# Layer 1's last group of hidden values: seven half-size products per half of the tokens in place of eight row pieces, and one comparison on ScalarE

## The chip, the cores and the metric

The kernel runs on one core of one Trainium2 chip, in one launch. The metric is device microseconds of that core, the median of the runs. Before the change it is 1847.09 us (three runs, 1846.87 to 1848.96).

A core has five engines that work side by side, each through its own queue in order: TensorE (PE, with its weight loads as PEld), VectorE (DVE), ScalarE (ACT), GpSimd (POOL) and SyncE (SP), whose queue here issues nearly all DMA transfers. Waits between engines are semaphore waits at the head of a queue, so that what stands behind a waiting instruction waits too.

## What is computed

Two layers over 2 x 1024 tokens of width 512, in fp32. Each layer adds to `x` an attention-like branch and an MLP-like branch of the normalised `x`. The change is in the last part, layer 1's second branch:

```python
def _sparsify_2to4(h):
    B, S, I = h.shape
    g = h.reshape(B, S, I // 4, 4)
    a = jnp.abs(g)
    _, idx = jax.lax.top_k(a, 2)
    pos = jnp.arange(4)
    mask = (pos == idx[..., 0:1]) | (pos == idx[..., 1:2])
    return (g * mask.astype(g.dtype)).reshape(B, S, I)
h = jax.nn.silu(jnp.einsum('bsh,hi->bsi', x, w_gate)) * jnp.einsum('bsh,hi->bsi', x, w_up)
h_sparse = _sparsify_2to4(h)
return jnp.einsum('bsi,ih->bsh', h_sparse, w_down)
```

So of every four neighbouring hidden values the two largest in size are kept, and the result is multiplied with `w_down` and added to `x`.

## The kernel before, in words

**Staging.** The kernel has three stages: layer 0 (pool `a`), layer 1's attention (pool `b`), and layer 1's second branch (pool `c`, from the end of attention on). Only the third matters here. `in_program_order` fixes each engine's order to the order in which the instructions are written, so the queues are an order written out by hand.

**The third stage.** The tokens are taken in two halves of 1024 (`pb`), and the 2048 hidden values in four groups of 512 (`g`). That makes eight groups, numbered 0 to 7 in the order of the work, and each is built by two of the 16 "units". A unit computes gate and up for 1024 tokens with seven products in place of eight (`gate_up`, line 179 for the matmuls, with a form of Strassen's method). Group 7 belongs to units 14 and 15, and is the last. `gate_up` calls `hook(0)` to `hook(6)` between its products; `put1(unit, at, ...)` hangs work of earlier groups into these hooks. What doesn't fit goes into the list `tail`, which is run after unit 15, item by item.

**Sparsification** (`sparsify`, L1385 to L1414) is a generator of twelve steps for one half of a group's tokens (512 of its 1024): the absolute value on ScalarE (L1399), then eleven on VectorE: the smaller of each pair (L1400), two comparisons within the pair (L1402, L1403), the larger (L1404), two comparisons across the pairs (L1406, L1407), their difference (L1408), two updates of the mask (L1409, L1410) and twice the multiplication of the hidden values with the mask (L1414, two of the four members each). `some_steps(n, half, count)` runs the next `count` steps.

**The down projection** comes in two forms:

- By seven products (`down_by_seven`, L246 to L325): for one half of the tokens, the hidden values and the weights are each cut into four quarters; sums of quarters are formed (of hidden values on VectorE, `hidden_first` and `hidden_last`, L265, L266, L272, L273; of weights on GpSimd, `down_weights`, L1373 to L1378), and seven products of 4 matmuls (128x256) are run (L297). Product 0 is copied by ScalarE (L304), product 1 added to it by VectorE (L307), which gives u2; products 2 to 6 are added to `x` by VectorE (L310), and u2 is added to three quarters of `x` by GpSimd (`add_u2`, L315). The products of a half take turns in two PSUM banks: `(m + half) % 2` for products 0, 1, 3 and 4, and 2, 5 and 6 go on in the bank of 0, 3 and 4.
- Row by row (`row_down`, L1454): for 128 tokens, four matmuls of 128x512 into one bank of the wide PSUM tiles, one addition to `x` by VectorE (L1459), and for the last group one store of these rows (L1462).

Groups 0 to 5 go by seven products in both halves. Group 6 goes by seven in half 0 and by four row pieces in half 1. Group 7 goes by eight row pieces. For group 6, `own_t3` (L1383) makes one weight difference apart, so that the weights themselves stay whole for the row pieces; it takes a tile of the tag `td1`, which has two buffers.

**The tail before** is the rest of group 6 (five products of half 0, each preceded by a row piece of half 1 as long as there are any), with the steps of group 7's sparsification between them by the list `steps`, and then group 7's eight row pieces, the first four on half 0 and the others on half 1.

Of the kernel before, what the change touches and what calls it, by code (L numbers as in the profile page):

```python
# [11 lines left out]
AF = mybir.ActivationFunctionType  # L12
ALU = mybir.AluOpType
# [22 lines left out]
def two_layers(ctx: ExitStack, tc: tile.TileContext, t: dict, out: bass.AP):  # L36
    nc = tc.nc
# [306 lines left out]
    with tc.tile_pool(name="a", bufs=1) as a:  # L344
# [382 lines left out]
        def quarters_w(n):  # L727

            return [w2_quarters[:, n % (NU // 2), c, e] for c in range(2) for e in range(2)]

        def down_weights(n, m):

            w11, w12, w21, w22 = quarters_w(n)
            if m == 0:
                td[n] = [
                    a.tile([P, 2, D // 2], F32, tag=f"td{k}", name=f"td{k}_{n}") for k in (1, 2, 4)
                ]
            t1, t2, t4 = (v.rearrange("p q (s d) -> p q s d", s=2) for v in td[n])
            if m == 0:
                if n < NU // 2:  # L740
                    nc.gpsimd.tensor_sub(w12, w22, w12)
                nc.gpsimd.tensor_add(t2, w12, w11)
            elif m == 1:
                nc.gpsimd.tensor_sub(t1, w22, t2)
            else:
                nc.gpsimd.tensor_sub(t4, w21, t2)

        hidden_first, hidden_last, down, products_of = down_by_seven(
            a, h0, td, quarters_w, lambda n: n // (NU // 2) * 2, in_place=True
        )  # L750
# [9 lines left out]
        for n in range(NU - 1):  # L760
            u = 2 * n + 2
            places = [range(7), range(7, 14)]
            if n == 0:
                places = [(7, 8, 8, 9, 9, 10, 10), (11, 12, 12, 13, 13, 14, 14)]
            elif n == 1:
                places = [range(1, 8), (8, 9, 10, 11, 12, 13, 13)]
            for half, at in enumerate(places):
                put0(u, at[0] - half, hidden_first, n, half)
                for f, *args in products_of(n, half):
                    if f == down:  # L770
                        place = at[args[2]]
                    put0(u, place + (f != down), f, *args)
                    if f == down and args[2] == 0:
                        put0(u, place, hidden_last, n, half)

            for m, (k, f) in enumerate(((1, 1), (3, 1), (6, 1))):
                at = places[1][k] + f
                put0(u, at, down_weights, n + 1, m)
        put0(2, 5, down_weights, 0, 0)
        put0(2, 6, down_weights, 0, 1)  # L780
        put0(2, 6, down_weights, 0, 2)

# [3 lines left out]
        for q, n in enumerate(((0, 2), (0, 4), (1, 2), (1, 4))):  # L786
            put0(*n, fwht_rows, q)
            for m in range(4):
                n, at = (0, (4, 5, 6, 6)[m]) if q == 0 else divmod(4 * q + 3 + m, 7)
# [11 lines left out]
        for base in (0, NU):  # L801
            i, d = 2 * base // NU, base + (1 if base else 3)
# [88 lines left out]
        n, second_half = NU - 1, list(products_of(NU - 1, 1))  # L891
# [14 lines left out]
    with tc.tile_pool(name="b", bufs=1, reuse_waits="tile") as b:  # L906
# [217 lines left out]
        held, sums = {}, {}  # L1124
# [86 lines left out]
        for u in range(len(units)):  # L1211

            for half in range(2):
                n = per * u - ahead + (3, 11)[half]
# [11 lines left out]
            for j in range(2):  # L1226
                n = per * u + 8 * j + 7
# [93 lines left out]
        n = len(second)  # L1321
# [14 lines left out]
    with tc.tile_pool(name="c", bufs=1, reuse_waits="tile") as c_:  # L1336
        units = [(pb, g, half) for pb in range(2) for g in range(G) for half in range(2)]
        groups = len(units) // 2
# [26 lines left out]
        def down_weights(n, last):  # L1365

            w11, w12, w21, w22 = quarters_w(n)
            if not last:
                td[n] = [
                    c_.tile([P, 2, D // 2], F32, tag=f"td{m}", name=f"td{m}_{n}", bufs=2)  # L1370
                    for m in (1, 2, 4)
                ]
                nc.gpsimd.tensor_sub(td[n][0], w12, w11)  # L1373
                nc.gpsimd.tensor_sub(td[n][1], w22, td[n][0])
            else:
                if n < groups - 2:
                    nc.gpsimd.tensor_sub(w12, w22, w12)
                nc.gpsimd.tensor_sub(td[n][2], w21, td[n][1])  # L1378

# [5 lines left out]
        def sparsify(n, half):  # L1385

            name = f"{n}_{half}"
            h = hs[n][:, :, :, half * TT // 2 : (half + 1) * TT // 2]
            ab = c_.tile([P, 4, TT], F32, tag="ab", name=f"ab_{name}")
            pair = ab.rearrange("p (q two) n -> p q two n", two=2)  # L1390
            hi = pair[:, :, 0]
            lo = c_.tile([P, 2, TT], F32, tag="lo", name=f"lo_{name}")
            first = c_.tile([P, 4, TT], BF16, tag="first", name=f"first_{name}")
            win = first.rearrange("p (q two) n -> p q two n", two=2)
            both = c_.tile([P, 2, TT], BF16, tag="both", name=f"both_{name}")
            way = c_.tile([P, TT], BF16, tag="way", name=f"way_{name}")
            wide = way.unsqueeze(1).to_broadcast([P, 2, TT])
            v = nc.vector
            yield nc.scalar.activation(ab.rearrange("p c (b n) -> p c b n", b=2), h, AF.Abs)  # L1399
            yield v.tensor_tensor(lo, pair[:, :, 0], pair[:, :, 1], ALU.min)  # L1400

            yield v.tensor_tensor(win[:, :, 0], pair[:, :, 0], pair[:, :, 1], ALU.is_ge)  # L1402
            yield v.tensor_tensor(win[:, :, 1], pair[:, :, 0], pair[:, :, 1], ALU.is_lt)  # L1403
            yield v.tensor_tensor(hi, pair[:, :, 0], pair[:, :, 1], ALU.max)  # L1404

            yield v.tensor_tensor(both[:, 0], lo[:, 0], hi[:, 1], ALU.is_ge)  # L1406
            yield v.tensor_tensor(both[:, 1], lo[:, 1], hi[:, 0], ALU.is_gt)  # L1407
            yield v.tensor_sub(way, both[:, 0], both[:, 1])  # L1408
            yield v.tensor_add(first[:, 0:2], first[:, 0:2], wide)  # L1409
            yield v.tensor_sub(first[:, 2:4], first[:, 2:4], wide)  # L1410
            for q in range(2):
                c = slice(2 * q, 2 * q + 2)
                f = first[:, c].rearrange("p c (b n) -> p c b n", b=2)
                yield v.scalar_tensor_tensor(h[:, c], f, 1.0, h[:, c], ALU.is_ge, ALU.mult)  # L1414
# [3 lines left out]
        def some_steps(n, half, count):  # L1418
            if (n, half) not in thinning:
                thinning[n, half] = sparsify(n, half)  # L1420
            for _ in range(count):
                next(thinning[n, half])

        hidden_first, hidden_last, down, products_of = down_by_seven(
            c_, hs, td, quarters_w, lambda n: 2 * units[2 * n][0]
        )
# [9 lines left out]
        between1, tail = {}, []  # L1436

        def put1(n, at, *what):

            between1.setdefault((n + at // 7, at % 7), []).append(what)  # L1440

        def sequence(n, half):

            for step in products_of(n, half):
                yield step
                if step[0] == down and step[3] > 4:
                    yield store, n, half, step[3] - 5
# [16 lines left out]
        for n in range(groups - 1):  # L1464
# [8 lines left out]
            for half, at in enumerate(((8, 11),) if end else (range(4, 11), range(11, 18))):  # L1473
                steps = list(sequence(n, half))
# [13 lines left out]


        n = groups - 1  # L1490
        rows = [(row_down, n - 1, i, j) for j in (2, 3) for i in range(2)]
        steps = [
            ((0, 2),), ((0, 1),), ((0, 2),), ((0, 2),), ((0, 3), (1, 1)), ((0, 2),), ((1, 1),),
            ((1, 1),), ((1, 2),), ((1, 2),), ((1, 2),), ((1, 3),),
        ]

        def go_on():
            for half, count in steps.pop(0) if steps else ():
                tail.append((some_steps, n, half, count))

        behind_last, tail = tail, []
        go_on()
        for what in behind_last:
            if what[0] == down and rows:
                tail.append(rows.pop(0))
                go_on()
            tail.append(what)
            if what[0] == down:
                go_on()
        for half in range(2):  # L1510
            for j in (2 * half, 2 * half + 1):
                for i in range(2):
                    tail.append((row_down, n, i, j))
                    go_on()

        tt, next_tt, second = None, None, None
        s_of = {}
# [117 lines left out]
```

## Time and profile before

| | us |
|---|---|
| median of three runs | 1847.09 |
| the profiled execution | 1850.59 |
| its span (first to last event on the core) | 1848.8 |
| TensorE busy in it | 1798.2 (97%) |
| VectorE busy | 1127.4 (61%) |
| GpSimd busy | 821.1 (44%) |
| ScalarE busy | 478.5 (26%) |
| mean granted TensorE clock, share of full | 0.994 |

The profile is of one execution; every time in it is counted from the span's start. In the lines of the timeline the columns are start, duration, engine, line of the kernel, operation, what is written and read (with the shape and type), the number of instructions merged, and in brackets the idle time before and what ended it. The chain of work that ended last is followed back from the last instruction. Rows of windows give, for a stretch, its length and then busy time and count of TensorE, its weight loads, VectorE, ScalarE and GpSimd, then the granted TensorE clock, the DMA share and GB/s. A matmul of fp32 is run as two instructions, so 4 matmuls are 8 of the profile's. Durations of successive instructions on VectorE and TensorE overlap by up to 0.2 us, so sums are made from start to start.

The last unit's gate and up products end at 1793.5, and the tail is run from 1794.8 on.

### The profile page before, as it was taken

To read this page: it belongs to the slowest core of one execution; us is meant where nothing else is said; L and a number is where in the kernel's file an instruction comes from. 1 tells how busy PE (TensorE), PEld (TensorE's weight loads), DVE (VectorE), ACT (ScalarE), POOL (GpSimd) and SP (SyncE) were. 2 spreads that over 40 slices of the span, in tenths; PEclk is the share of its full clock that TensorE was granted. 3 is DMA by queue.
4 is the path that set the end of the run, shared out by engine and by line. 5 is a ranking of instruction groups with operands and counts; after the bars stand their busy time and mean duration, and the time that the engine had idled before them with its cause. 6 is when DMAs were issued, how large, how long until landed. Compare 5 with 4: busy or idle time off the path is not lost.

```text
span 1848.8 us, 18896 instructions
## 1 busy us (share of the span) xinstructions
PE 1798.2 (97%) x7348; PEld 918.6 (50%) x7348; DVE 1127.4 (61%) x1464; ACT 478.5 (26%) x683; POOL 821.1 (44%) x711
## 2 busy tenths in 40 slices
PE   6999999999999999999999999999999999999999
PEld 4446565655655564333333333333455555555544
DVE  3685444565543438565657656642768678768665
ACT  2322222122221102334333443412211221212120
POOL 4335364246552222467667756732244244343410
PEclk9999999999999999999999999999999999999999
DMA  6121111011101100000001000011101101211101
GB/s 228 35 80 34 35 35 38 31 46 35 35 23 34 35 7 23 1 12 12 13 1 35 12 12 1 24 46 34 35 23 57 57 23 58 91 35 46 46 1 46
DMA packets 29465, 68.12 MB, mean 37 GB/s; under 512 B 3392, under 2 KB 11584, under 8 KB 27840
## 3 DMA queue, kind: packets, MB, share of 16 engines
q1 hardware_dynamic: 28656, 66.61, 10.9%
q8 instruction: 59, 0.97, 0.2%
q10 hardware_dynamic: 720, 0.30, 0.1%
q14 instruction: 30, 0.25, 0.0%
HBM read 62.70 MB, written 4.19 MB: 36 GB/s over the span
## 4 chain that ended last, share of the span: by engine, by line
PE 88%; DVE 5%; POOL 2%; ACT 2%; issue 2%; DMA 1%; ACTq 0%; POOLq 0%; DVEq 0%
PE p_a L179 20%; PE p_c L179 19%; PE d L297 19%; PE pq L990 6%; PE m L1042 4%; PE s L1095 4%; PE o L1137 3%; PE po L990 3%; PE pv L990 3%; PE dr L1454 2%; POOL acc L1145 2%; PE w L1157 1%; DVE tops L1050 1%; PE pp L579 1%; PE s L1101 1%
## 5 line engine op out<-in xcount | busy, mean ns | idle before, releaser
L315 POOL TENSOR_TENSOR x<-x,de 128x512 f32<-128x512 f32 x87 | 125.9, 1462 | 298.4 <-DVE x L310 163.7
L1145 POOL TENSOR_TENSOR acc<-acc,pt 128x1024 f32<-128x1024 f32 (+3 forms) x138 | 233.7, 1719 | 0.0
L1050 DVE TENSOR_REDUCE tops<-m 128x2 f32<-128x1024 f32 (+2 forms) x192 | 180.8, 956 | 49.1 <-PE m L1042 44.7
L310 DVE TENSOR_TENSOR x<-x,d 128x512 f32<-128x512 f32 x145 | 99.3, 685 | 149.8 <-PE d L297 148.6
L1112 ACT ACTIVATE pt<-s 128x1024 f32<-128x1024 f32 (+3 forms) x160 | 115.1, 766 | 180.3 <-PE s L1101 167.1
L297 PE MATMUL d<-td,h 128*128 128x256 f32 x592 | 139.9, 380 | 2.2 <-DVE h L272 2.2
L297 PEld LDWEIGHTS d<-td,h 128*128 128x128 f32 x592 | 112.2, 190 | 46.2 <-issue 29.0
L990 PE MATMUL pq<-xt,wqk 128*128 128x512 f32 x256 | 125.1, 617 | 0.8 <-ACT qk L1006 0.8
L179 PE MATMUL p_a<-t_a,s_a 128*128 128x512 f32 x256 | 119.2, 610 | 2.1 <-DVE t_a L156 2.1
L179 PE MATMUL p_a<-xt,w 128*128 128x512 f32 x256 | 117.7, 603 | 0.7 <-ACT xt L136 0.7
L179 PE MATMUL p_c<-xt,s_c 128*128 128x512 f32 x256 | 115.2, 593 | 2.5 <-DVE e_c L224 1.4
L179 PE MATMUL p_a<-xt,s_a 128*128 128x512 f32 x256 | 116.6, 598 | 0.0
L179 PE MATMUL p_c<-xt,gu 128*128 128x512 f32 x256 | 114.9, 592 | 0.0
L179 PE MATMUL p_c<-t_c,s_c 128*128 128x512 f32 x256 | 114.6, 592 | 0.0
L1049 DVE TENSOR_TENSOR m<-m,mask 128x256 f32<-128x256 f32 x128 | 54.7, 427 | 98.2 <-PE m L1042 93.7
L1042 PE MATMUL m<-qk,qk 32*128 32x512 f32 (+3 forms) x768 | 107.7, 536 | 3.6 <-ACT acc L1112 3.0
L1095 PE MATMUL s<-qk,qk 32*128 32x512 f32 (+3 forms) x768 | 93.8, 532 | 3.7 <-ACT pt L1112 2.3
L172 POOL TENSOR_TENSOR s_c<-gu,s_c 128x512 f32<-128x512 f32 x16 | 20.4, 1275 | 135.9 <-PE p_c L179 135.9
L1117 POOL TENSOR_SCALAR_AFFINE_SELECT pt<-pt 128x256 f32<-128x256 f32 x112 | 48.4, 448 | 71.2 <-ACT pt L1112 70.6
L990 PEld LDWEIGHTS pq<-xt,wqk 128*128 128x128 f32 x256 | 44.5, 191 | 66.5 <-issue 62.1
L179 PEld LDWEIGHTS p_a<-xt,s_a 128*128 128x128 f32 x256 | 47.2, 190 | 57.1 <-issue 56.7
L179 PEld LDWEIGHTS p_c<-xt,s_c 128*128 128x128 f32 x256 | 48.5, 190 | 54.2 <-issue 52.9
(240 smaller groups left out, 3049.2 us busy)
## 6 DMA issues: line engine op xcount, KB each, us to landing
w<-in_W SPq DMA_DIRECT2D x32, 512.0 KB, 3.6
gu<-in_gu SPq DMA_DIRECT2D x32, 512.0 KB, 3.6
wd<-in_down SPq DMA_DIRECT2D x8, 1024.0 KB, 4.8
x<-in_x SPq DMA_DIRECT2D x16, 256.0 KB, 4.2
w2h<-in_W2q SPq DMA_DIRECT2D x4, 1024.0 KB, 11.7
xr<-in_x SPq DMA_DIRECT2D x16, 256.0 KB, 2.7
wqk<-in_WqkvT SPq DMA_DIRECT2D x16, 256.0 KB, 3.2
out_x<-x SPq DMA_DIRECT2D x16, 256.0 KB, 2.0
```

What stands on the lines that cost most here:

```text
L179: nc.tensor.matmul(pair[:, m, :], a[:, m, k, :], x[:, k, :], start=start and k == 0, stop=stop and k == 1, skip_group_check=True,)
L297: nc.tensor.matmul(out_[:, j, :], lhs[:, q, j * P : (j + 1) * P], rhs[:, q], start=m in (0, 1, 3, 4) and j == q == 0, stop=j == q == 1, sk ...
L310: nc.vector.tensor_add(r, r, out_)
L315: nc.gpsimd.tensor_add(r, r, u2[half])
L990: nc.tensor.matmul(got[0], lhs(k), rhs(k), start=(k == 0), stop=(k == KC - 1))
L1042: nc.tensor.matmul(pair[h // 2][:, h % 2, :e], q[rows, qt * P : (qt + 1) * P], k[rows, c * 512 : c * 512 + e], start=True, stop=True,)
L1049: nc.vector.tensor_add(d, d, mask.unsqueeze(1).to_broadcast([P, 2, P]))
L1050: nc.vector.tensor_reduce(out=tops[u][:, c, qt, 2 * p : 2 * p + 2], in_=pair[p][:, :, :e], axis=mybir.AxisListType.X, op=ALU.max,)
L1095: nc.tensor.matmul(pair[h // 2][:, h % 2, s:], k[rows, kt * P : (kt + 1) * P], q[rows, cols], start=True, stop=False,)
L1112: nc.scalar.activation(pt[:, :, s:], pair[p][:, :, s:], AF.Exp, scale=1.0 / math.sqrt(HD))
L1137: nc.tensor.matmul(po[rows, s:], v[:, rows], pts[h // 2][:, h % 2, s:], start=(kt == 0), stop=last, tile_position=(0, h * HD),)
L1145: eng.tensor_add(acc[:, :, s:], acc[:, :, s:], pt[:, :, s:])
```

## The change

Four edits:

1. Group 7 is put through the seven products in both halves. In place of the eight row pieces, the items of `sequence(7, 0)` and `sequence(7, 1)` go to the tail, behind those of group 6, with the steps of the sparsification and the sums of the hidden values between them by the list `between_items`.
2. The weight differences of group 7 (four GpSimd operations) are put at hooks 3 and 4 of unit 15. The condition that leaves out the third of them is now true of group 6 alone.
3. In group 7's sparsification the second comparison (`is_lt`) is made on ScalarE as 1 minus the first one.
4. The stores of the last group come two at a time, after product 5 (both row pieces of one block) and after product 6 (of the other), in place of one after each row piece.

```diff
-                if n < groups - 2:
+                if n != groups - 2:
                     nc.gpsimd.tensor_sub(w12, w22, w12)
...
-            yield v.tensor_tensor(win[:, :, 1], pair[:, :, 0], pair[:, :, 1], ALU.is_lt)
+            if n == groups - 1:
+                yield nc.scalar.activation(
+                    win[:, :, 1], win[:, :, 0], AF.Copy, bias=1.0, scale=-1.0
+                )
+            else:
+                yield v.tensor_tensor(win[:, :, 1], pair[:, :, 0], pair[:, :, 1], ALU.is_lt)
...
         n = groups - 1
+        for last in range(2):
+            put1(2 * n + 1, 3 + last, down_weights, n, last)
         rows = [(row_down, n - 1, i, j) for j in (2, 3) for i in range(2)]
-        steps = [
-            ((0, 2),), ((0, 1),), ((0, 2),), ((0, 2),), ((0, 3), (1, 1)), ((0, 2),), ((1, 1),),
-            ((1, 1),), ((1, 2),), ((1, 2),), ((1, 2),), ((1, 3),),
+        sums = [[(f, n, half)] for half in range(2) for f in (hidden_first, hidden_last)]
...
+        between_items = [
+            thin((0, 2)), thin((0, 1)), thin((0, 2)), thin((0, 2)), thin((0, 3), (1, 1)),
+            thin((0, 2)), thin((1, 1)), thin((1, 1)), sums[0], sums[1],
+            thin((1, 2)), thin((1, 2)), thin((1, 1)), thin((1, 1)), thin((1, 1)),
+            thin((1, 1)), thin((1, 1)), sums[2] + sums[3],
         ]
...
-        for what in behind_last:
+        for what in behind_last + list(sequence(n, 0)) + list(sequence(n, 1)):
             if what[0] == down and rows:
                 tail.append(rows.pop(0))
                 go_on()
             tail.append(what)
             if what[0] == down:
                 go_on()
-        for half in range(2):
-            for j in (2 * half, 2 * half + 1):
-                for i in range(2):
-                    tail.append((row_down, n, i, j))
-                    go_on()
```

The order of the instructions in the changed kernel, engine by engine, is known before it is run. On VectorE, from the first `L1414` of group 7's half 0 on, it is: L1414 twice, the addition of group 6's product 4, L1400 of half 1, the last row piece's addition, L1402, the addition of product 5, L265, L266, the addition of product 6, L272, L273, L1404, and then group 7's L307 and L310 with the rest of half 1's steps between them. On GpSimd, the four weight differences of group 7 stand directly ahead of the three L315 of group 6. (Line numbers here are those of the kernel before; those above 1403 are up to 8 higher after the change.)

More of the change, by code (lines that the diff above doesn't have):

```diff
@@ L1490, in two_layers, with thin @@
         n = groups - 1
+        for last in range(2):
+            put1(2 * n + 1, 3 + last, down_weights, n, last)
         rows = [(row_down, n - 1, i, j) for j in (2, 3) for i in range(2)]
-        steps = [
-            ((0, 2),), ((0, 1),), ((0, 2),), ((0, 2),), ((0, 3), (1, 1)), ((0, 2),), ((1, 1),),
-            ((1, 1),), ((1, 2),), ((1, 2),), ((1, 2),), ((1, 3),),
+        sums = [[(f, n, half)] for half in range(2) for f in (hidden_first, hidden_last)]
+        def thin(*steps):
+            return [(some_steps, n, half, count) for half, count in steps]
+        between_items = [
[3 more added lines that the diff above has]
+            thin((1, 1)), thin((1, 1)), sums[2] + sums[3],
         ]
         def go_on():
-            for half, count in steps.pop(0) if steps else ():
-                tail.append((some_steps, n, half, count))
+            tail.extend(between_items.pop(0) if between_items else ())
         behind_last, tail = tail, []
         go_on()
-        for what in behind_last:
+        for what in behind_last + list(sequence(n, 0)) + list(sequence(n, 1)):
             if what[0] == down and rows:
```

## The prediction

> **What bounds the kernel now.** I read the page's busy shares first (PE 97%), then the chain that ended last, in order of time, because the change touches only the last 55 us. Its end:
>
> ```profile
> 1810.58 3.43 PE dr L1454 x8
> 1814.01 3.45 PE d L297 x16
> 1817.46 27.48 PE dr L1454 x64
> 1844.94 0.02 issue
> 1844.97 0.69 DVE x L1459
> ```
>
> TensorE sets the end without a gap: from 1817.3 the eight row pieces of group 7 run 27.4 us back to back, then one VectorE addition and one store. Dividing, a row piece (8 instructions) takes 27.48/8 = 3.43 us and a product (8 instructions of 256 columns) 3.45/2 = 1.73 us. VectorE is not late: its last comparison work ends at 1828.0, and then it only waits for TensorE. So the tail is worth what TensorE does there, as long as nobody else gets late. Next I read the timeline by engine, to see what the added VectorE and GpSimd work would meet:
>
> ```profile
> 1743.22 2.18 POOL L315 TENSOR_TENSOR x<-x,de 128x512 f32<-128x512 f32 x1 [8.52 <-DVE x L310]
> ...
> 1744.19 2.29 DVE L1403 TENSOR_TENSOR first<-ab 128x1024 bf16<-128x1024 f32 x1
> ...
> 1745.36 2.25 POOL L1383 TENSOR_TENSOR td<-wd 128x512 f32<-128x512 f32 x1
> ...
> 1746.52 2.18 DVE L1404 TENSOR_TENSOR ab<-ab 128x1024 f32<-128x1024 f32 x1
> ...
> 1748.73 1.64 DVE L1406 TENSOR_TENSOR both<-lo,ab 128x512 bf16<-128x512 f32 x1
> ...
> 1770.86 1.22 DVE L1403 TENSOR_TENSOR first<-ab 128x1024 bf16<-128x1024 f32 x1
> ```
>
> The same L1403 takes 1.22 us alone and 2.29 us beside GpSimd. The ends tell why: L315 ends at 1745.40, L1403 at 1746.48 (1.1 later), L1383 at 1747.61 (1.1 later), L1404 at 1748.70 (1.1 later). They take turns: each GpSimd operation of 128x512 costs VectorE 1.12 us when VectorE's own operation reads two SBUF inputs. A VectorE addition from PSUM does not take part: L1459 at 1814.05 takes 0.69 us in the middle of a GpSimd addition (1812.52 to 1814.71).
>
> **The change part by part.** All sums are against the profiled execution (span 1848.8 us, its time 1850.59); the median of the runs is 1847.09, 3.5 less, and I carry the difference over to it.
>
> TensorE's work: out go 8 row pieces x 3.43 = 27.4 us, in come 14 products x 1.73 = 24.2 us: -3.2 us. This is the whole possible gain.
>
> The comparison (L1403, 1.13 us from start to start) leaves VectorE twice. No ScalarE row shows the new operation; near ones are the copy of 128x1024 (1.01 us) and the absolute value of 128x2048 (1.91 us): at least 1.0, at most 1.9, and I take 1.0, the nearer size. ScalarE is idle from 1798 to 1806, so in half 0 it is done by 1803 and wanted at 1807; behind it waits only the absolute value of half 1, which waits for L1407 anyway. In half 1 it stands behind the copy of product 0 and is done a few us before its use. Cost 0, at 1.9 too. The gain in half 0 is only 0.3 us, since VectorE then waits for the second row piece of group 6 (its sum can be read at 1803.7, not before).
>
> GpSimd: four weight differences of group 7 are new. The first, td1, takes the buffer of group 6's td1 (two buffers; td3 of group 6 took the other), whose last reader is product 3 of group 6. That ends at 1805.26 and is visible at 1805.46. So the four can't run early under the gate and up products; they run from 1805.5, and the three additions of group 6's u2 (L315), two of which now run at 1788.5, queue behind them: seven GpSimd operations in the stretch where VectorE finishes half 0's mask. Taking turns at 1.12 us each, by the order in which the queues stand: td1 until 1806.7, VectorE's way until 1807.1, td2 until 1808.2, the first mask update until 1808.8, the third difference until 1809.9, the second update until 1810.5, td4 until 1811.6, the first L1414 until 1812.7, addition 1 until 1813.8, the second L1414 until 1815.0, addition 2 until 1816.1, half 1's L1400 until 1817.2, addition 3 until 1818.3, L1402 until 1819.4. Between these stand the PSUM additions of group 6, 0.6 each.
>
> Then, in VectorE's order: the addition of product 5 of group 6 (1820.0), two sums of half 0's hidden values (0.6 and 0.72), the addition of product 6 of group 6 (ends 1821.9), two more hidden sums (until 1823.2). Before, that product 6 was added at 1818.85. This matters now: product 0 of group 7 goes into the same PSUM bank as products 4 and 6 of group 6 (half 0 uses bank 0 for 0, 2, 4 and 6 in both groups), so TensorE waits for that addition, while the row pieces went to other banks. TensorE starts group 7 at 1821.95 instead of 1817.30: **+4.65 us**.
>
> Half 0 then needs 7 x 1.73 = 12.1 us, and once about 0.35 us more, where product 4 waits for the addition of product 2, which stands behind half 1's comparisons and two u2 additions. It ends at 1834.4. The products alternate between two banks, so each waits for the VectorE read two products back (0.9 us, within 1.73 us): hidden, else a stall at every product.
>
> Half 1 can't begin until its mask is applied. Its last L1414 stands behind the addition of half 0's product 6: visible 1834.7, added by 1835.3, L1414 until 1836.4. Product 1 needs three hidden sums more (0.60 + 0.72 + 0.72): 1838.5. TensorE would have been ready for it at 1834.4 + 1.73 = 1836.2: **+2.4 us**. Then 6 x 1.73 = 10.4 us: TensorE ends at 1848.9, where it now ends at 1844.75. Sum: -3.2 + 4.65 + 0.35 + 2.4 = **+4.15 us**.
>
> Store: now the last addition releases one transfer (issue 0.33 us), after it two (0.82 us for a pair earlier in this kernel): **+0.5 us**. The earlier stores stay covered by the products.
>
> TensorE's clock: the row first. The windows of the trace with granted clock (the column ahead of the last two):
>
> ```profile
> 30.00:31.00 1.00, 1.00 (x8) 0.82 (x8) 0.00 (x0) 0.34 (x1) 0.00 (x0) 0.99 0.75 307
> 31.00:32.00 1.00, 0.06 (x1) 0.00 (x0) 0.24 (x1) 0.73 (x2) 0.00 (x0) 0.50 0.15 61
> 36.00:37.00 1.00, 1.00 (x3) 0.48 (x2) 0.00 (x0) 0.00 (x0) 0.00 (x0) 0.50 0.00 0
> 37.00:38.00 1.00, 1.00 (x2) 0.35 (x2) 0.00 (x0) 0.00 (x0) 0.00 (x0) 0.59 0.00 0
> ```
>
> After a stretch of small matmuls and a gap of 2.08 us the clock is halved from 31.0 to 37.8, and eight matmuls of 512 columns take 5.99 us instead of 3.60. The Trainium skill, "TensorE: Matmul & The Clock Gate", Part 1, says that the array is slowed after a whole idle window of about 3.4 us and restored after a busy one, with windows that run free. By that rule a gap of 4.65 us holds a whole idle window in (4.65 - 3.41)/3.41 = 36% of cases, and the sum gets an estimated 0.4 us. The trace is harsher: the window ahead of 31.0 was not idle, and the one after it, busy for its last 1.3 us of 3.4, did not restore the clock. By the trace a gap of 4.65 us nearly always leaves a window mostly empty. Then half speed lasts from 1.1 to over 4 us of the work behind the gap, half of it lost: 1.0 to 2.3 us by the phase. I go by the row: **+1.5 us**. Half 0's products pace VectorE there, so nothing hides it.
>
> Total: 4.15 + 0.5 + 1.5 = +6.1 us: a span of 1854.9, a median of 1853.2.
>
> **The rivals.** (a) All waits as summed, but the clock holds: +4.65, 1851.7. For it: later gaps of 1.1 to 1.4 us left the clock at full. Against: they are much shorter. 19%.
>
> (b) Taking turns costs GpSimd and not VectorE: the additions of group 6 are then in time. VectorE's chain without GpSimd, with its PSUM waits: product 6 of group 6 is added by 1818.3; TensorE starts at 1818.4, half 0 ends at 1830.5, half 1's mask at 1832.5, product 1 of half 1 at 1834.6 and the end at 1845.0. With the store +0.7: 1847.8. Against: L1403 and L1404 above, where VectorE paid. 12%.
>
> (c) Not slower: the products stay back to back, since the bank wait and the mask are met. TensorE's -3.2 comes through, the pair of stores costs 0.5: -2.7, 1844.4. The deciding point is whether product 6 of group 6 is added before 1817.5, the moment its sum can be read, and half 1's mask is applied before 1829.4. Before, that addition was made at 1818.85 and that mask ended at 1828.0 with less work in front of it. 4%.
>
> (d) A second slowing of the clock in the gap between the halves (2.0 us, then 0.7 us), or more lock turns than counted: about +9, 1856. 7%.
>
> The main case has 58%. That the change does not do what it says would mean products that never start before the rows would have ended; the order in which the instructions stand excludes it.
>
> **How the numbers follow.** 0.2% is 3.7 us, about what a measurement of this kernel can tell from no change. The main case and (d) are slower by more; of (a) most, since 4.65 lies 1 us above the bound; (b) and (c) are within it, as even TensorE's full saving is below 3.7 us. Slower 0.81, same 0.16, faster 0.03. The range leaves out (c) and a part of (b), and the far end of (d): 1848.8 to 1856.0; the main case alone is 1851.8 to 1855.2.
>
> **What would show it.** In the profile after: L315 of group 6 near 1812 to 1818, not at 1788; VectorE rows of 1.6 to 2.3 us at L1414 and L1400 of half 0; a TensorE wait for VectorE's L310 of 4 to 5 us ahead of group 7's first product; a granted clock near 0.5 for 2 to 4 us behind it; and a TensorE wait of 2 us for L1419 or L272 between the halves. I am wrong if group 7 starts within 1.5 us of 1817.3, or if VectorE's rows stay at 1.22 us beside GpSimd.

## The result, and the profile after

The changed kernel takes 1858.32 us (median of six runs, 1854.76 to 1859.87) beside 1848.31 us before (six runs, 1846.87 to 1849.49): a ratio of 1.0054, 95% interval 1.0043 to 1.0064, that is 10.0 us slower. Five more runs of it later gave 1.0045 (1.0033 to 1.0058), 8.3 us. The forecast of slower was right; its time, 1853.2, and the upper end of its range, 1856.0, were too low. Part of that is the base: the three runs shown before have a median of 1847.09, the six 1848.31.

From one execution to another the start of the tail moves (1792.5 to 1795.7 in the profiles below), because the clock is halved for a while in earlier stages, differently each time (20.5 us of half speed ahead of the tail in the profile before, 27.3 in the one after). So I compare profiles by the **tail**: from the first row piece of group 6 to the end of the span. It is 1848.8 - 1794.83 = 53.97 us before and 1858.1 - 1795.72 = 62.38 us after, 8.41 us longer. (The span is printed to 0.1 us, so a tail is good to 0.05 us.)

TensorE in the tail of the changed kernel, by the timeline (group 6's last product, then group 7's products 0, 1 and 2):

```profile
1816.47 1.90 PE L297 MATMUL d<-td,h 128*128 128x256 f32 x8
1822.72 3.78 PE L297 MATMUL d<-wd,h 128*128 128x256 f32 x8 [4.36 <-DVE x L310]
1826.30 3.06 PE L297 MATMUL d<-td,sd 128*128 128x256 f32 x8
1829.20 1.89 PE L297 MATMUL d<-wd,h 128*128 128x256 f32 x8
```

The wait for L310, the addition of group 6's product 6, is there: from 1816.47 + 1.73 = 1818.20 to 1822.72, 4.52 us. But behind it product 0 takes 3.58 us to the next start and product 1 2.90 us, where 1.73 is the rule. What VectorE did until then, from the same timeline:

```profile
1808.05 1.57 DVE L1414 TENSOR_TENSOR first<-first,way 128x1024 bf16<-128x1024 bf16 x1
1809.54 1.75 DVE L1415 TENSOR_TENSOR first<-first,way 128x1024 bf16<-128x1024 bf16 x1
...
1811.81 3.90 DVE L1419 SCALAR_TENSOR_TENSOR h<-first,h 128x1024 f32<-128x1024 bf16 x2
...
1816.24 1.70 DVE L1400 TENSOR_TENSOR lo<-ab 128x1024 f32<-128x1024 f32 x1
...
1821.99 0.68 DVE L310 TENSOR_TENSOR x<-x,d 128x512 f32<-128x512 f32 x1
```

L1414 and L1415 are the two mask updates here, and L1419 is the multiplication with the mask. The same work before (L1409, L1414, L1400, and then the addition of product 6):

```profile
1806.86 0.69 DVE L1409 TENSOR_TENSOR first<-first,way 128x1024 bf16<-128x1024 bf16 x1
...
1809.49 2.35 DVE L1414 SCALAR_TENSOR_TENSOR h<-first,h 128x1024 f32<-128x1024 bf16 x2
...
1812.36 1.22 DVE L1400 TENSOR_TENSOR lo<-ab 128x1024 f32<-128x1024 f32 x1
...
1818.85 0.68 DVE L310 TENSOR_TENSOR x<-x,d 128x512 f32<-128x512 f32 x1
```

So a mask update took 0.69 us and takes 1.57 to 1.75, two multiplications took 2.35 and take 3.90, and L1400 took 1.22 and takes 1.70. The reason stands on GpSimd:

```profile
1806.39 1.27 POOL L1373 TENSOR_TENSOR td<-wd 128x512 f32<-128x512 f32 x1 [38.05 <-PE d L297]
...
1812.39 6.67 POOL L315 TENSOR_TENSOR x<-x,de 128x512 f32<-128x512 f32 x3
```

The first weight difference waited 38 us for a product of group 6 that still read the buffer of td1, and all seven operations fall between 1806.4 and 1819.1. The TensorE clock comes on top (windows of 2 us; the granted clock is the third number from the end):

```profile
1820.00:1822.00 2.00, 0.00 (x0) 0.00 (x0) 1.97 (x5) 0.00 (x0) 0.00 (x0) 0.96 0.00 0
...
1824.00:1826.00 2.00, 2.00 (x6) 1.55 (x6) 1.13 (x1) 0.00 (x0) 0.00 (x0) 0.50 0.00 0
...
1828.00:1830.00 2.00, 2.00 (x9) 1.75 (x8) 0.51 (x1) 0.08 (x1) 0.00 (x0) 0.83 0.00 0
```

0.96 and 0.83 say where it was halved: a drop to 0.5 makes 0.96 if it comes 0.16 us ahead of 1822, and 0.83 if it lasts 0.67 us past 1828. The halved stretch runs from 1821.84 to 1828.67, that is 6.83 us. Between the halves TensorE waits as forecast, first for the mask, then for a hidden sum:

```profile
1838.97 0.67 PE L297 MATMUL d<-wd,h 128*128 128x256 f32 x2 [0.35 <-DVE h L1419]
1840.62 1.56 PE L297 MATMUL d<-wd,h 128*128 128x256 f32 x6 [0.97 <-DVE h L1419]
1842.89 1.96 PE L297 MATMUL d<-td,sd 128*128 128x256 f32 x8 [0.71 <-DVE sd L272]
```

### The profile page after: what moved, and what is told of

Read it like the earlier page. It is cut to its first block, busy times and chain, and to the rows that moved or that the text cites. A ratio compares the mean times of both kernels' runs of the same rounds, so it can differ in the third digit from the quotient of the medians.

```text
span 1858.1 us, 19032 instructions
## 1 busy us (share of the span) xinstructions
PE 1801.4 (97%) x7396; PEld 929.6 (50%) x7396; DVE 1135.4 (61%) x1474; ACT 481.4 (26%) x687; POOL 835.0 (45%) x721
## 4 chain that ended last, share of the span: by engine, by line
PE 86%; DVE 6%; POOL 3%; ACT 2%; issue 2%; DMA 0%; DVEq 0%; ACTq 0%; POOLq 0%
PE p_a L179 20%; PE d L297 19%; PE p_c L179 19%; PE pq L990 6%; PE m L1042 4%; PE s L1095 4%; PE o L1137 3%; PE po L990 3%; PE pv L990 3%; POOL acc L1145 2%; PE w L1157 1%; DVE tops L1050 1%; PE pp L579 1%; PE s L1101 1%; ACT acc L1112 1%
## 5 line engine op out<-in xcount | busy, mean ns | idle before, releaser
L315 POOL TENSOR_TENSOR x<-x,de 128x512 f32<-128x512 f32 x93 | 136.3, 1481 | 280.5 <-DVE x L310 147.5
L310 DVE TENSOR_TENSOR x<-x,d 128x512 f32<-128x512 f32 x155 | 106.0, 684 | 155.7 <-PE d L297 154.5
L297 PE MATMUL d<-td,h 128*128 128x256 f32 x624 | 147.5, 380 | 2.2 <-DVE h L272 2.2
L297 PEld LDWEIGHTS d<-td,h 128*128 128x128 f32 x624 | 118.1, 190 | 47.1 <-issue 29.2
L179 PEld LDWEIGHTS p_a<-t_a,s_a 128*128 128x128 f32 x256 | 49.3, 198 | 53.7 <-issue 53.0
L1042 PEld LDWEIGHTS m<-qk,qk 32*128 32x128 f32 x768 | 43.8, 184 | 64.1 <-PE s L1101 21.9
```

What stands on the lines that cost most here:

```text
L179: nc.tensor.matmul(pair[:, m, :], a[:, m, k, :], x[:, k, :], start=start and k == 0, stop=stop and k == 1, skip_group_check=True,)
L297: nc.tensor.matmul(out_[:, j, :], lhs[:, q, j * P : (j + 1) * P], rhs[:, q], start=m in (0, 1, 3, 4) and j == q == 0, stop=j == q == 1, sk ...
L310: nc.vector.tensor_add(r, r, out_)
L315: nc.gpsimd.tensor_add(r, r, u2[half])
L1042: nc.tensor.matmul(pair[h // 2][:, h % 2, :e], q[rows, qt * P : (qt + 1) * P], k[rows, c * 512 : c * 512 + e], start=True, stop=True,)
```

## The experiments

My theory: GpSimd's work, pushed into the tail by a buffer, takes turns with VectorE and delays the addition that frees a PSUM bank; the TensorE gap that this opens then halves the clock. The main rival: the seven products themselves cost it, because VectorE has more to do for them. The table has the tail of each profile, the gap ahead of group 7 (behind product 0 in other_bank and own_buffer_bank), what the halved clock cost (the work behind the gap against its length at full clock), and the measured ratio.

| kernel | tail, us | against before | gap | clock loss | ratio (95% interval) |
|---|---|---|---|---|---|
| before | 53.97 | | 0 | 0 | |
| after | 62.38 | +8.41 | 4.52 | 3.02 | 1.0054 (1.0043 to 1.0064) |
| after_again | 61.71 | +7.74 | 4.53 | 2.33 | 1.0045 (1.0033 to 1.0058) |
| seven_dve | 61.48 | +7.51 | 4.62 | 1.78 | 1.0053 (1.0039 to 1.0067) |
| act_only | 53.94 | -0.03 | 0 | 0 | 1.0003 (0.9993 to 1.0014) |
| own_buffer | 56.21 | +2.24 | 1.21 | 0 | 1.0022 (1.0014 to 1.003) |
| own_buffer_bank | 54.82 | +0.85 | 0.18 | 0 | 1.0005 (0.9996 to 1.0013) |
| other_bank | 58.09 | +4.12 | 3.49 | 0 | 1.0026 (1.0017 to 1.0035) |
| filled | 59.52 | +5.55 | filled | 0 | 1.0038 (1.0024 to 1.0052) |
| gap_short | 58.07 | +4.10 | 2.28 | 1.80 | 1.0021 (1.0012 to 1.0029) |
| gap_long | 61.18 | +7.21 | 4.67 | 2.51 | 1.0036 (1.0024 to 1.0049) |
| rows_then_seven | 53.13 | -0.84 | 0 | 0 | 0.9994 (0.9986 to 1.0002) |

**own_buffer.** The changed kernel with one line of `own_t3` different:

```diff
-            td[n].append(c_.tile([P, 2, D // 2], F32, tag="td1", name=f"td3_{n}", bufs=2))
+            td[n].append(c_.tile([P, 2, D // 2], F32, tag="td3", name=f"td3_{n}", bufs=1))
```

> Only change to the changed kernel: group 6's extra weight difference gets a buffer of its own, so that group 7's four weight differences find a free buffer early. My theory (GpSimd's work pushed into the tail delays the addition that frees the PSUM bank, and the long TensorE gap then halves its clock): the four run near 1767 to 1773, the three L315 of group 6 as before the change, group 7's first product starts about 1.1 us after group 6's last instead of 4.5 us, the granted clock stays at 1.00, and the time is 1847 to 1850, some 8 to 10 us below the changed kernel. Rival (the seven-product form itself costs it, by VectorE's hidden sums and additions and the two PSUM banks): at most 2 us below the changed kernel, 1855 to 1858.

Measured: 1852.44 us, ratio 1.0022: about 6 us below the changed kernel's 1.0054. In the profile the four differences run from 1765.5 to 1772.8, VectorE's mask work takes what it took before, and TensorE's gap is short:

```profile
1765.48 1.27 POOL L1373 TENSOR_TENSOR td<-wd 128x512 f32<-128x512 f32 x1
...
1804.72 0.69 DVE L1414 TENSOR_TENSOR first<-first,way 128x1024 bf16<-128x1024 bf16 x1
...
1807.56 2.35 DVE L1419 SCALAR_TENSOR_TENSOR h<-first,h 128x1024 f32<-128x1024 bf16 x2
...
1813.64 1.89 PE L297 MATMUL d<-td,h 128*128 128x256 f32 x8
1816.58 1.99 PE L297 MATMUL d<-wd,h 128*128 128x256 f32 x8 [1.05 <-DVE x L310]
1818.41 1.89 PE L297 MATMUL d<-td,sd 128*128 128x256 f32 x8
```

The gap is 1.21 us from 1815.37, with products of 1.73 to 1.83 us behind it. So the moved GpSimd work was 3.3 us of the gap and, through the clock, 2 to 3 us more. The rival's "at most 2 us" falls. But the time is 2 to 5 us above what I expected. The gap between the halves (2.7 us) and the pair of stores (0.7 us) remain, and the 1847 to 1850 us had left too little for them. And the median's 4.1 us is 1.8 us more than the profile's 2.24, which lies just outside the interval of 2.6 to 5.5 us.

**filled.** Between group 6's last product and group 7's first:

```diff
+        def keep_busy(count):
+            bank = ps_wide("fill")[:, 0, :]
+            for r in range(count):
+                nc.tensor.matmul(
+                    bank, hs[6][:, r % 4, 1, 384:512], wd[6][:, r % 4, :],
+                    start=True, stop=True, skip_group_check=True,
+                )
+
+        at = next(k for k, w in enumerate(tail) if w[0] == down and w[1] == n)
+        tail.insert(at, (keep_busy, 5))
```

> The changed kernel with five matmuls of 128x512 into an unused PSUM bank, never read, between group 6's last product and group 7's first: 4.3 us of TensorE work inside a gap of 4.5 us, no wait removed. My theory: the granted clock stays at 1.00 behind the gap, group 7's first two products take 1.73 us each instead of 3.6 and 2.9, and the time is about 3 us below the changed kernel (near 1855), with a smaller spread from run to run. Rival (the halved clock is an accident of the one profiled run, or hidden under VectorE's pace): within 0.5 us of the changed kernel.

Measured: 1855.63 us, ratio 1.0038 (1.0024 to 1.0052), beside 1.0054 and 1.0045 of the changed kernel. These intervals overlap, so the times alone do not show the 3 us. The profile does, since no wait was removed in it:

```profile
1816.86 4.45 PE L1527 MATMUL fill<-wd,h 128*128 128x512 f32 x10
1821.39 1.99 PE L297 MATMUL d<-wd,h 128*128 128x256 f32 x8
1823.22 1.89 PE L297 MATMUL d<-td,sd 128*128 128x256 f32 x8
```

Product 0 begins as late in the tail as in the changed kernel (27.0 us from its start in both) and takes 1.83 us instead of 3.58. The tail is 2.86 us shorter than after's and 2.19 shorter than after_again's, which is what the halved clock cost there (3.02 and 2.33). The smaller spread did not show (1853.05 to 1858.86): the kernel before, without a gap, spreads as far (1844.33 to 1853.14).

**seven_dve.** The changed kernel with the `is_lt` on VectorE in every group.

> The changed kernel with both comparisons on VectorE again (the ScalarE edit undone). My theory: in half 0 VectorE's 1.1 us falls partly into its 0.9 us wait for a row piece, so 0.2 to 0.4 us there; in half 1 it stands behind the hidden sums, where VectorE waits for TensorE for 4 us. 0 to +1 us against the changed kernel. Rival (the comparison is what the VectorE-bound tail lives on): +2 us or more.

Measured: 1857.93 us, 1.0053, the same as after. Without the clock losses the tails are 59.70 and 59.36 us: the ScalarE step is worth 0.3 us, less than the times can tell.

**act_only.** The kernel before with that step alone.

> The kernel before with the ScalarE comparison alone, in group 7. TensorE is gapless in its tail and both masks are ready in time, so my theory says no change: within 1 us of the kernel before. Rival (the ScalarE step brings a wait of its own that counts): 2 us slower or more.

Measured: 1848.9 beside 1848.73 us, no difference, and a tail of 53.94 us beside 53.97. These two runs say that the comparison is not what makes the changed kernel slower.

**gap_short and gap_long.** The kernel before, with one VectorE operation of 128x512, or two of 128x1024, on hidden values that the first row piece of group 7 reads (the values stay as they are):

```diff
+        def same(width):
+            x = hs[groups - 1][:, :, 0, 0:width]
+            nc.vector.tensor_tensor(x, x, x, ALU.max)
+
+        at = next(k for k, w in enumerate(tail) if w == (down, n - 1, 0, 6))
+        tail.insert(at, (same, 128))
...
+        tail[at + 1 : at + 1] = [(same, 256), (same, 256)]
```

> The kernel before with one extra VectorE operation (the larger of a value and itself, 128x512, in place on the hidden values that the first row piece of group 7 reads), put behind L1404 of half 1: it opens a TensorE gap of about 2.2 us ahead of group 7 and adds no other wait. If only a gap of more than about 3.4 us halves the clock: +2.2 us, granted clock 1.00. If a window partly empty is enough: +2.2 to +4 us, with a granted clock of 0.5 in some of it.

> The kernel before with two such operations of 128x1024 behind the addition of group 6's product 6: a TensorE gap of about 4.5 us ahead of group 7, as long as the changed kernel's, with rows and not products behind it. Theory (the gap halves the clock and the restart takes up to 6.8 us): +4.5 us and 1.5 to 3.4 us more, +6 to +8 us, with a granted clock of 0.5 behind the gap, and a spread between runs above the kernel before. Rival (the clock plays no part): +4.5 us.

Measured: 1.0021 (3.9 us) and 1.0036 (6.7 us). The row pieces are one group in the timeline. gap_short:

```profile
1816.48 1.89 PE L297 MATMUL d<-td,h 128*128 128x256 f32 x8
1820.49 29.43 PE L1454 MATMUL dr<-wd,h 128*128 128x512 f32 x64 [2.12 <-DVE h L1518]
```

and gap_long:

```profile
1814.36 1.89 PE L297 MATMUL d<-td,h 128*128 128x256 f32 x8
1820.76 30.14 PE L1454 MATMUL dr<-wd,h 128*128 128x512 f32 x64 [4.51 <-DVE h L1518]
```

Before, the same 64 instructions took 27.63 us. So 2.28 us of waiting costs 4.1 us, and 4.67 us costs 7.2. The clock part (1.80 and 2.51 us) is of the size that it has with products behind the gap (1.78 to 3.02).

**other_bank.** The changed kernel with a free wide bank for product 0 of half 0:

```diff
+        def down_wide(n, half, m):
+            down(n, half, m, ps_wide(f"dw_{n}_{half}_{m}")[:, 0, :])
+
+        tail = [(down_wide, *w[1:]) if w[0] == down and w[1:] == (n, 0, 0) else w for w in tail]
```

> The changed kernel with product 0 of group 7's half 0 in a wide PSUM bank that is free, so that it doesn't wait for the addition of group 6's product 6. My theory: the gap moves behind product 0, since product 1 needs a hidden sum that stands behind the same addition; product 1 starts at about the same time less the 1.7 us of product 0, and the shorter gap costs less clock: 1.5 to 4 us below the changed kernel. Rival (the bank wait alone is the loss): 6 us or more below it, near 1851.

Measured: 1853.02 us, 1.0026, 5.2 us below after: more than I expected, less than the rival.

```profile
1815.70 1.89 PE L297 MATMUL dw<-wd,h 128*128 128x256 f32 x8
1820.92 1.97 PE L297 MATMUL d<-td,sd 128*128 128x256 f32 x8 [3.33 <-DVE sd L272]
```

The gap moved behind product 0 as expected, 3.49 us long, and product 1 starts earlier by nearly product 0's length. What I had not expected is that in this execution the clock held. The runs spread from 1847.32 to 1856.51, so it need not hold in all of them.

**own_buffer_bank.** The edits of own_buffer and other_bank together.

> Both the own buffer and the free bank. My theory: no gap between group 6 and group 7, the clock stays at 1.00, only the gap between the halves (about 2.4 us) and the pair of stores are left against TensorE's saving of 3.2 us: within 1.5 us of the kernel before, and about 1 us below the own buffer alone. Rival (the products are paced by VectorE and not by TensorE): 3 us or more above the kernel before.

Measured: 1849.13 us, 1.0005 (0.9996 to 1.0013): the kernel before, within what can be told. The gap is 0.18 us. With the same number of products and hidden sums as the changed kernel, 9 of its 10 us are gone; the rival falls. (Product 2 goes on in the bank of product 0, so this edit also takes the wait inside half 0 from 0.55 to 0.25 us.)

**after_again.** The changed kernel once more.

> The changed kernel as it is, once more, for a second profile and more runs beside the kernel before. Theory (the gap ahead of group 7 is a fixed 4.4 us of waits, and what the halved clock costs behind it depends on where the gap falls in windows of 3.4 us that run free): the waits and the order of the records the same to 0.1 us, the tail from the first row piece to the end of the span 5.4 us longer than before plus a clock loss between 1.0 and 3.4 us, that is 60.4 to 62.8 us; median 8 to 10 us above the kernel before. Rival (the loss in the first profile was the rule): 62.4 us again and a halved stretch of 6.8 us.

Measured: 1857.16 us, 1.0045; tail 61.71 us, gap 4.53 us, and behind it:

```profile
1819.49 3.78 PE L297 MATMUL d<-wd,h 128*128 128x256 f32 x8 [4.36 <-DVE x L310]
1823.07 2.38 PE L297 MATMUL d<-td,sd 128*128 128x256 f32 x8
```

The wait is 4.36 us to the hundredth as in the first profile; the clock cost 1.85 + 0.48 = 2.33 us instead of 3.02. The waits are the same in both profiles, the clock loss is not.

**rows_then_seven.** The kernel before with half 0 of group 7 by row pieces and half 1 by seven products:

```diff
+        for last in range(2):
+            put1(2 * n + 1, 3 + last, down_weights, n, last)
+        put1(2 * n + 1, 4, own_t3, n)
...
-        for half in range(2):
-            for j in (2 * half, 2 * half + 1):
-                for i in range(2):
-                    tail.append((row_down, n, i, j))
-                    go_on()
+        for j in range(2):
+            for i in range(2):
+                tail.append((row_down, n, i, j))
+                go_on()
+                if j == 1 and i == 0:
+                    tail += [(hidden_first, n, 1), (hidden_last, n, 1)]
+        tail += list(sequence(n, 1))
```

and `own_t3` with a tag and two buffers of its own.

> The kernel before with group 7's half 0 by row pieces, as it is, and its half 1 by seven products; the weight differences at hooks 3 and 4 of the last unit with buffers of their own, both comparisons on VectorE. Half 1's mask was applied at 1828.0 in the kernel before, 3 us ahead of the end of half 0's row pieces, so its three hidden sums fit in. My theory (the products are worth their 1.6 us of TensorE where VectorE has the time ahead of them): no TensorE gap in the tail, clock at 1.00, the tail 0.9 us shorter than before (-1.6 for the products, +0.7 for the pair of stores), so 0 to 1.5 us faster than the kernel before, hardly to be told from it by the median. Rival (seven products pace themselves by VectorE and lose in any place): 1 us slower or more, with gaps between the products.

Measured: 1847.5 us beside 1848.23, ratio 0.9994 (0.9986 to 1.0002): not to be told from before, by the median. The profile has no gap:

```profile
1816.64 13.90 PE L1454 MATMUL dr<-wd,h 128*128 128x512 f32 x32
1830.38 1.89 PE L297 MATMUL d<-wd,h 128*128 128x256 f32 x8
1832.11 1.89 PE L297 MATMUL d<-td,sd 128*128 128x256 f32 x8
```

The tail is 53.13 us, 0.84 us shorter than before where 0.9 was worked out. In this place the products bring what they save, which is little.

## Why the prediction was right or wrong

**Right: the work.** 14 products came in at 1.73 us each where the clock was full: -3.2 us.

**Right: the gap ahead of group 7.** +4.65 forecast, 4.52 measured, by the path named: td1's buffer, seven GpSimd operations between VectorE's, the addition of product 6, the PSUM bank. own_buffer shows the GpSimd part (gap 1.21 us), own_buffer_bank that the bank and the order of VectorE's work are the rest (0.18 us). Rival (b), that VectorE would not pay, fell with the rows of 1.57 to 1.75 us.

**Right, a little small: the other terms.** Inside half 0 the wait was 0.55 us for 0.35; between the halves 2.70 for 2.4; the pair of stores 0.68 for 0.5 (the last addition ends 3.82 us ahead of the end of the span, 3.14 before). With 0.1 us in all for TensorE's restarts, which I had put at nothing, that is about 0.8 us more than forecast.

**Wrong: the clock.** "I go by the row: +1.5 us", from "1.0 to 2.3 us by the phase". The three profiles with this gap lost 3.02, 2.33 and 1.78 us, 2.4 on average, and filled gives 2.86 us of the tail back. The step that failed is the length of the half speed, "from 1.1 to over 4 us of the work behind the gap": for it to end after 1.1 us of work, a window in which the work only begins again must restore the clock at its end. The runs show otherwise. In the first profile the window from the drop at 1821.84 to 1825.25 was busy from 1822.72 on, 2.53 of 3.41 us, and the clock stayed halved for another whole window. In all five tails with a drop it came back only behind a window that TensorE filled. So at least 3.41 us of work run at half speed, and the least loss is 1.7 us: 1.5 lay below it. By the windows in the last section a gap like this one costs 1.7 to 3.4 us by where it lies, 2.5 on the mean (an estimate from the measured gap, the length of the windows and the busy time below which the clock fell there).

The forecast's own figures were weaker than they looked, too. Half of 1.1 us is 0.55 and not 1.0. And the gap of 2.08 us begins at 31.05, behind the drop at 31.0, so that row showed how long the clock can stay down, and not what gap brings it down.

This was also the place where the Trainium skill ("TensorE: Matmul & The Clock Gate", Part 1) was weighed. By its whole idle window the clock would have fallen in 36% of the cases; it fell in all three profiles. gap_short contradicts that rule: 2.28 us of waiting, less than a window, were enough. That a busy window restores the clock is what all five tails show.

Together: -3.2 + 4.5 + 0.55 + 2.7 + 0.7 + 0.1 + 3.0 = 8.4 us in the first profile, against 6.1 forecast; the tail says 8.41. Of the 2.3 us between, 1.5 are the clock. The measured 10.0 and 8.3 us have intervals (7.9 to 11.8 and 6.1 to 10.7 us) that hold 8.4. The range failed because its upper end stood at the "far end" of a second slowing, which did not come, instead of the first one's own size, and because it was tied to three runs whose median lay 1.2 us below that of six.

**Open.** In own_buffer and filled too the median is 1.5 to 1.8 us above what the tail of the profile gives. The gaps between the halves are not likely to be the reason: they put at most 1.7 us of waiting into 3.4 us, in seven_dve the clock held through 1.82, and own_buffer_bank has these gaps too, where profile and median agree (0.85 and 0.9 us). The runs of both kernels have a lower granted clock on the mean (0.9940 and 0.9938) than those of the kernel before (0.9948), but act_only's, with an unchanged tail, have 0.9941. So the time ahead of the tail may differ by chance; no profile shows it.

## What to carry to other kernels

Before moving work to a queue "where it is idle", look for the buffer that it writes: a tile whose last reader is late pulls the work to that reader, here by 38 us, into the one stretch where its neighbour is busy. Cost a TensorE gap at its length, and from about 2 us on add the halved clock behind it: 1.8 to 3.0 us in the five profiles in which it fell, nothing in the one in which a gap of 3.49 us lay well. A form that saves 12% of TensorE's work pays only where its sums are finished ahead of it; in the tail that was the second half of the tokens behind the first one's rows, and it brought 0.84 us in the profile, too little for the medians to tell.

## What the runs showed of the hardware

In each profile all changes of the granted clock lie whole multiples of 3.4133 us apart; before, for example, it falls at 30.99 and comes back at 1324.64, and 1293.65 us are 379 times that. So time can be divided into windows of that length, and where these fall in the tail differs from profile to profile. Here are tails divided at these places. The number behind the length is the time for which TensorE was busy. First after:

```profile
1818.42:1821.84 3.42, 0.00 (x0) 0.00 (x0) 3.39 (x5) 0.00 (x0) 0.64 (x1) 1.00 0.00 0
1821.84:1825.25 3.41, 2.53 (x6) 2.08 (x7) 3.25 (x5) 0.00 (x0) 0.00 (x0) 0.50 0.00 0
1825.25:1828.66 3.41, 3.41 (x9) 2.69 (x9) 0.00 (x0) 1.54 (x2) 0.00 (x0) 0.50 0.00 0
```

then the window ahead of the drop in after_again, and the one in gap_short:

```profile
1813.81:1817.22 3.41, 1.32 (x7) 0.81 (x5) 3.41 (x4) 0.00 (x0) 2.02 (x1) 1.00 0.00 0
```

```profile
1817.39:1820.81 3.42, 1.30 (x6) 0.82 (x5) 3.38 (x5) 0.00 (x0) 0.00 (x0) 1.00 0.00 0
```

the two windows of the gap in seven_dve, of which the first did not bring the clock down and the second did:

```profile
1816.43:1819.85 3.42, 1.59 (x8) 1.06 (x6) 3.42 (x4) 0.00 (x0) 2.29 (x2) 1.00 0.00 0
1819.85:1823.26 3.41, 0.89 (x4) 0.81 (x5) 3.34 (x6) 0.00 (x0) 0.00 (x0) 1.00 0.00 0
```

and the two in other_bank, where it held:

```profile
1815.87:1819.29 3.42, 1.72 (x8) 1.16 (x7) 3.38 (x5) 1.54 (x2) 0.69 (x1) 1.00 0.00 0
1819.29:1822.70 3.41, 1.78 (x8) 1.63 (x9) 3.31 (x5) 0.00 (x0) 0.00 (x0) 1.00 0.00 0
```

The clock fell at the end of a window with 1.32 us of work or less (0, 0.89, 1.30 and 1.32, and 0.85 in gap_long) and held behind 1.59, 1.72 and 1.78. In these tails, then, the line lies between 1.32 and 1.59 us of TensorE work in 3.41, and what counts is how a gap falls into the windows: 3.49 us split between two passed, 2.28 us inside one did not. It can fall after the work has begun again: in seven_dve group 7 starts at 1822.38 and the clock falls at 1823.26. It came back only behind a window that TensorE filled; 1.14 us (after_again), 1.46 (gap_long) and 2.53 (after) were not enough. So the halved stretches are 3.41 us (gap_short, seven_dve) or 6.83 us (after, after_again, gap_long) long, nothing between. This line does not hold for all matmuls: in the rows of the prediction the clock fell at 31.0 although TensorE, on small matmuls, was busy all through the last microsecond before.
